# Layer 1's softplus in two parts, and one more sum step at its bias products

## The chip, the cores and the metric

The kernel runs on one core of one Trainium2 chip. The metric is the device time of one execution in microseconds; several executions of a kernel are timed and their median is compared. A core has five instruction queues that work side by side: TensorE (PE in the profile; its weight loads are PEld), VectorE (DVE), ScalarE (ACT), GpSimd (POOL) and SyncE (SP), which here only issues DMAs. Each takes its own instructions strictly in order and waits for the others through semaphores.

## The reference, cut to what matters

The program computes two residual layers on x, of shape (8, 256, 96, 96) in float32. Each layer first applies a group norm without weights, over groups of 8 channels. Layer 0 is an attention over channels in the Fourier domain. Layer 1, where the change is made, is a linear attention:

```python
def _L1_conv_ref(x, Wq, bq, Wk, bk, Wv, bv):
    xf = x.reshape(B, C, N)                                  # N = 9216 pixels
    q = softplus(einsum('dc,bcn->bnd', Wq, xf) + bq)         # d = 32
    k = softplus(einsum('dc,bcn->bdn', Wk, xf) + bk)
    v = einsum('ec,bcn->ben', Wv, xf) + bv
    attn_map = einsum('bdn,ben->bde', k, v)
    k_sum = sum(k, axis=-1) + 1e-6
    norm = 1.0 / einsum('bnd,bd->bn', q, k_sum)
    return einsum('bnd,bde,bn->ben', q, attn_map, norm)

x = x + _L0_conv_ref(_gn(x), ...)
x = x + _L1_conv_ref(_gn(x), ...)
```

The kernel never forms v. It forms k times the transposed x, with a column of ones for the sum of k, and applies the weights of v to that small matrix.

## The kernel before, in words

The eight images are worked off one after another in the loop at L1027, numbered from 0. An image goes through three stages. `images` applies the layer-0 attention to the rotated image, row block by row block, and adds the result to x. `layer1` does the group norm and all of layer 1 up to the small matrices. `output` forms the layer-1 result and stores it. In `output`, `attention` and `rotate` of the next image are mixed in.

A fifth activity runs beside these: `pair_sums` of the next image, a generator of 37 steps after its start. It loads x in a grouped layout, turns it by 32x32 blocks on VectorE (`turn_blocks`, L369), stores the turned rows to DRAM for a later stage (L372, SyncE, one store of 1536 KB for two turns), adds and subtracts row pairs (`pair`, L391 on GpSimd, L392 on VectorE for even pairs and on GpSimd for odd ones), and multiplies on TensorE into two accumulators (`products`, L343). A step is named (u, q): u counts row pairs from 0 to 12, q the three parts of a pair. The step (u, 0) also issues pair u + 1, and (u, 1) also issues turn u + 2, in both cases ahead of its own products. Turns with an even number write one half of the area of turned rows and those with an odd number the other half; the store behind each odd turn reads both halves. An odd turn also issues the loads of a later grouped block.

All engines run in the order in which the program text issues the instructions: the whole is built in a manual schedule, with no planner. `weave` (L929) sets how the sum steps fall in: a stage is a generator, and each number that it yields is the count of sum steps to be issued at that place (fractions are added up within a stage). `images` issues the start and 22 steps, so `layer1` begins with (7,1) and (7,2) in its group norm, and (8,0) between the two parts of the variance product. Image 7 is the last and has no sum steps.

`layer1` before the change, in its order:

- L773 to L787: group norm, weights of k and q scaled (`wkq`, L779 on ScalarE), bias products (`l1b`, L784 on TensorE), biases `bkqs` (L787 on VectorE).
- L805 to L822: projection. For each of six sets s, and for c = 0 (k) and c = 1 (q), 16 matmul instructions of 384 columns fill one PSUM tile that holds four column blocks of 32 channels. VectorE writes max(z, 0) (L814), ScalarE writes exp(-|z|) (L816 Abs, L817 Exp). In s = 1 VectorE also scales the weights of v (L821, L822).
- L829 to L844: `softplus(c, s)`. With e = exp(-|z|), softplus is max(z, 0) + log(1 + e). VectorE forms u = 1 + e (L834) and its rounding error (L835), ScalarE takes Ln of u (L836), VectorE subtracts the error (L837), and `close` adds the logarithm later (L843). softplus(0, 0) stands ahead of two sum steps and of the `bvs` product (L861).
- L864 to L891: for each set s, three transposes of k (`kT`, L867) and ScalarE's copy of them (L868), then softplus(0, s + 1); and for each of its three i, eight transposes of x into two PSUM tiles (`xT`, L878), their copies to SBUF (L881 on ScalarE, L883 on VectorE), `close`, and from s = 3 on softplus of q in two of the three. Twelve products `kx` (L850, two instructions each) for three i at a time accumulate k times x.
- L896 to L926: `kxs`, the transposed small matrices and the denominators, with three more sum steps, (9,0) to (9,2).

PSUM tiles of the name `ps` take turns in five buffers; a sixth tile waits until the first is read. All of `l1b`, `kq`, `bvs`, `kT` and `xT` are such tiles.

```python
        ex = y_of(b)[:, :, LO:LO + NS * CH]
...
            k, i = ((s // 2, s % 2) if s < 4 else (0, s - 2)) if c == 0 else ((1, s + 2) if s < 4 else (0, s))
```

`ex` holds e for k and q, `kq(c, s)` holds max(z, 0) and then the softplus, both in free space of the other image's area.

## Time and profile before

| | |
|---|---|
| median of 3 runs | 2661.95 us (2651.09 to 2665.03) |
| the profiled execution | 2650.85 us |
| its span, first to last instruction | 2649.0 us |
| mean granted TensorE clock | 0.984 |
| TensorE busy | 2509.3 us, 95% |
| VectorE busy | 1789.0 us, 68% |
| ScalarE busy | 1155.9 us, 44% |
| GpSimd busy | 865.6 us, 33% |
| `kq` products L812 | 127.9 us for the eight images |
| `xT` transposes L878 | 148.4 us |
| `kx` products L850 | 96.9 us (52.9, 23.9 and 20.1) |
| projection in image 0 | begins at 350.05 us |
| first `kT` and last `kx` in image 0 | 370.52 us and 403.03 us |

A line of a group gives line, engine, operation, output and inputs with the count, then the busy time and the mean in ns, then the idle time of the engine just before these instructions and what ended most of it. In a view in order of time, a line begins with start and duration in us and ends with the idle time before it and its releaser in brackets. In a table of windows the entries are the busy time of each engine with its instructions, then the granted share of TensorE's clock, the DMA share and GB/s. A busy TensorE is not a TensorE at its peak. Rows of one engine can overlap a little[...].

### The profile page before, as it was taken

Reading aid. Unit: us, or ns where it says so; the run is one execution under the profiler, and the core shown is the slowest. Engines: PE = TensorE matmul, PEld = TensorE weight load, DVE = VectorE, ACT = ScalarE, POOL = GpSimd, SP = SyncE. Lnnn points to the kernel's source line nnn. Section 1 sums busy time; section 2 is a strip of 40 time slices with the busy share of each in tenths; the row PEclk is TensorE's granted clock in tenths of the full one; section 3 lists DMA queues with packets and bytes.
Section 4 is the critical chain, followed back from the end, with each engine's and each line's share of the span. In section 5 each row is a group of like instructions: output and inputs, shape, how many; then the busy total and the mean of one; then the engine's idle time right before and its main releaser. Section 6 shows DMA issues by size and latency. Waiting matters only on the chain. (4 is left out here: it accounts for less than half of the span.)

```text
span 2649.0 us, 41157 instructions
## 1 busy us (share of the span) xinstructions
PE 2509.3 (95%) x15580; PEld 1730.2 (65%) x15580; DVE 1789.0 (68%) x3449; ACT 1155.9 (44%) x1985; POOL 865.6 (33%) x817
## 2 busy tenths in 40 slices
PE   3799999999999999999999999999999999999987
PEld 3775666757677576766668566685666757667544
DVE  3457866577756777568675686757866678766766
ACT  0035353453634526344353544435354353534554
POOL 2213514136042451324422343223523135141311
PEclk8899999999999999999999999999999999999999
DMA  9872628637195461935629264492636826286003
GB/s 210 238 216 60 166 71 270 205 67 189 40 313 161 106 173 57 315 120 143 153 90 305 80 167 129 159 316 42 166 89 230 245 60 179 58 289 210 1 7 144
DMA packets 282797, 413.27 MB, mean 156 GB/s; under 512 B 40772, under 2 KB 208872, under 8 KB 282600
## 3 DMA queue, kind: packets, MB, share of 16 engines
q1 hardware_dynamic: 274304, 406.16, 53.2%
q10 hardware_dynamic: 8296, 4.49, 0.8%
q8 instruction: 123, 2.02, 0.3%
q14 instruction: 74, 0.61, 0.1%
HBM read 256.72 MB, written 153.86 MB: 155 GB/s over the span
## 5 line engine op out<-in xcount | busy, mean ns | idle before, releaser
L710 PE MATMUL z<-arena,mz 128*128 128x384 f32 (+1 forms) x2304 | 593.4, 491 | 0.0
L718 PE MATMUL po<-e,wo 128*128 128x384 f32 x1536 | 527.6, 487 | 1.7 <-ACT e L755 1.7
L754 POOL TENSOR_TENSOR e<-e 128x768 f32<-128x768 f32 x192 | 348.4, 1815 | 552.7 <-ACT e L753 529.3
L343 PE MATMUL acc<-eo 128*128 128x257 f32 (+2 forms) x2368 | 437.1, 336 | 50.0 <-POOL eo L382 23.0
L343 PEld LDWEIGHTS acc<-eo 128*128 128x128 f32 (+1 forms) x2368 | 383.8, 194 | 143.9 <-issue 42.4
L710 PEld LDWEIGHTS z<-arena,mz 128*128 128x128 f32 (+1 forms) x2304 | 310.5, 164 | 236.0 <-issue 51.9
L718 PEld LDWEIGHTS po<-e,wo 128*128 128x128 f32 x1536 | 290.0, 190 | 204.7 <-ACT e L755 7.2
L749 DVE TENSOR_TENSOR e<-z,xT 128x768 f32<-128x768 f32 x384 | 361.9, 950 | 75.4 <-PE z L710 74.9
L647 PEld LDWEIGHTS y<-tm,arena 96*128 96x128 f32 x3072 | 365.9, 195 | 52.9 <-issue 18.9
L647 PE MATMUL y<-tm,arena 96*128 96x128 f32 x3072 | 385.7, 281 | 15.3 <-DMA arena<-xtd 6.4
L753 ACT ACTIVATE e<-e 128x1536 f32<-128x1536 f32 x192 | 284.5, 1482 | 195.2 <-DVE e L749 193.3
L391 POOL TENSOR_TENSOR eo<-arena 128x768 f32<-128x768 f32 x88 | 184.5, 2096 | 536.3 <-DVE arena L369 473.2
L720 DVE TENSOR_TENSOR arena<-arena,po 128x384 f32<-128x384 f32 x384 | 209.9, 553 | 190.0 <-PE po L718 190.0
L755 ACT ACTIVATE e<-e 128x768 f32<-128x768 f32 x192 | 162.0, 844 | 367.1 <-POOL e L754 363.2
L986 POOL TENSOR_TENSOR arena<-arena,po 128x384 f32<-128x384 f32 x180 | 179.1, 1014 | 224.0 <-ACT po L985 224.0
L369 DVE STREAM_TRANSPOSE arena<-arena 128x768 f32<-128x768 f32 x192 | 175.7, 953 | 32.5 <-DMA xtd<-arena 23.0
L299 DVE BATCH_NORM_STATS2 st<-arena 128x6 f32<-128x384 f32 x384 | 194.4, 548 | 0.0
L654 ACT COPY ys<-y 128x4 f32<-128x4 f32 (+1 forms) x200 | 32.4, 162 | 363.8 <-DVE arena L653 363.7
L878 PE MATMUL xT<-ident,arena 128*128 128x128 f32 x1152 | 148.4, 277 | 10.0 <-ACT xT L881 9.6
L878 PEld LDWEIGHTS xT<-ident,arena 128*128 128x128 f32 x1152 | 127.2, 142 | 32.0 <-issue 13.6
L985 ACT COPY po<-o 128x384 f32<-128x384 f32 x180 | 79.0, 485 | 157.4 <-PE o L977 152.4
L653 DVE COPY arena<-y 128x384 f32<-128x384 f32 (+1 forms) x200 | 109.1, 546 | 40.8 <-PE y L647 38.6
(225 smaller groups left out, 2493.1 us busy)
## 6 DMA issues: line engine op xcount, KB each, us to landing
xtd<-arena SPq DMA_DIRECT2D x48, 1536.0 KB
arena<-xtd SPq DMA_DIRECT2D x192, 384.0 KB
arena<-in_x_dram SPq DMA_DIRECT2D x96, 768.0 KB
out_dram<-arena SPq DMA_DIRECT2D x192, 384.0 KB
arena<-in_x_dram SPq DMA_DIRECT2D x376, 192.0 KB
tm<-rx SPq DMA_DIRECT2D x96, 159.0 KB
wl<-in_w1t_dram SPq DMA_DIRECT2D x8, 256.0 KB
wl<-in_w2t_dram SPq DMA_DIRECT2D x8, 256.0 KB
```

Of the source, the lines that this page charges most:

```text
L299: nc.vector.bn_stats(out=st[:, k, c, :], in_=x_of(b)[:, k, c * CH:(c + 1) * CH])
L343: nc.tensor.matmul(acc[c][:, m * (C + 1):m * (C + 1) + C + 1 - m * P], lhsT=eo[0:np_, q, c, 1 + m * P:1 + (m + 1) * P], rhs=eo[0:np_, q, c ...
L391: nc.gpsimd.tensor_add(e, ft, gt)
L647: nc.tensor.matmul(pu[:, o:o + P], lhsT=xt[:, s, k * P:(k + 1) * P], rhs=tm[:, n:n + P], start=True, stop=True)
L710: nc.tensor.matmul(out[:, 0:CH].rearrange("p (h q) -> p h q", q=PR), lhsT=columns(mz, k, c, j), rhs=yz[:, k, f, :, o:o + PR], start=(k == ...
L718: nc.tensor.matmul(po[:, 0:CH], lhsT=wo[:, k, m * P:(m + 1) * P], rhs=e[:, k, :], start=(k == 0), stop=(k == KC - 1))
L720: nc.vector.tensor_add(x[:, m, n], x[:, m, n], po[:, 0:CH])
L749: nc.vector.tensor_add(e[:, 2 * c:2 * c + 2, :].rearrange("p t (q h) -> p t q h", h=H), pz[:, 0:CH].rearrange("p (h q) -> p q h", h=H).uns ...
L753: nc.scalar.activation(e, e, AF.Square)
L754: nc.gpsimd.tensor_add(e[:, 0:2, :], e[:, 0:2, :], e[:, 2:4, :])
L878: nc.tensor.transpose(pt[:, j * C + k * P:j * C + (k + 1) * P], x[:, k, o:o + P], ident)
L986: nc.gpsimd.tensor_add(x[:, m, r], x[:, m, r], t)
```

## The change

The softplus is cut into `part` (all VectorE work but the last addition, now with the error subtracted from max(z, 0) at once) and `log` (ScalarE's Ln with bias 1, written over e). The temporary u is now VectorE's alone.

- The first parts of k move into the projection: `part(0, s - 1)` stands behind the two L814 of set s, and `part(0, 5)` behind the loop. `log(0, 0)` stands ahead of it. The small ScalarE instruction that made a zero bias goes away.
- The transposes of k move within a set: from ahead of its three i to the last one (i % 3 = 2), behind `close`, and ahead of that i's transposes of x. `log(0, s + 1)` follows the copy of kT on ScalarE, `part(1, s)`, the first part of q, follows on VectorE, and `log(1, s)` stands behind that i's copies. `close` is called once in a set.
- VectorE takes 12 of the 36 copies of `xT` in an image (the first tile of each i with i % 3 below 2), before 6.
- `layer1` yields one more sum step, between the scaling of `wkq` and the bias products. So every later sum step comes one place earlier, and one fewer is left for `output`.
- In `images` the yield is written the other way round, with the same values.

```diff
--- before.py
+++ after.py
@@ -758,7 +758,7 @@
             if len(pending) > 2:
                 project(*pending.pop(0))
             if i >= WI:
-                yield 2.5 if i > WI else 1
+                yield 1 if i == WI else 2.5
         for p in pending:
             yield 1
             project(*p)
@@ -777,6 +777,7 @@
         nc.sync.dma_start(out=wvs, in_=wvt.rearrange("(k p) o -> p k o", p=P))
         for k in range(KC):
             nc.scalar.activation(wkq[:, k], wkq0[:, k], AF.Copy, scale=rstd[:, k:k + 1])
+        yield 1
         pb = ps_tile(f"l1b_{b}")
         for c in range(2):
             for k in range(KC):
@@ -801,6 +802,14 @@
             k, i = ((s // 2, s % 2) if s < 4 else (0, s - 2)) if c == 0 else ((1, s + 2) if s < 4 else (0, s))
             o = LO + NS * CH + i * CH
             return y_of(b)[:, k, o:o + CH]
+
+        def part(c, s):
+
+            z, e = kq(c, s), ex[:, c, s * CH:(s + 1) * CH]
+            u = two.tile([P, CH], F32, tag="v16", name=f"spu_{b}_{c}_{s}")
+            nc.vector.tensor_scalar_add(u, e, 1.0)
+            nc.vector.scalar_tensor_tensor(u, in0=u, scalar=1.0, in1=e, op0=ALU.subtract, op1=ALU.subtract)
+            nc.vector.tensor_sub(z, z, u)
 
         for s in range(NS):
             n = slice(s * CH, (s + 1) * CH)
@@ -815,32 +824,26 @@
                                         op0=ALU.add, op1=ALU.max)
                 nc.scalar.activation(ex[:, c, n], ps[:, 0:CH], AF.Abs, bias=bkqs[:, c:c + 1])
                 nc.scalar.activation(ex[:, c, n], ex[:, c, n], AF.Exp, scale=-1.0)
+            if s:
+                part(0, s - 1)
             if s == 1:
                 nmb = own[:, 0:C].rearrange("p (k n) -> p k n", k=KC)
                 for k in range(KC):
                     nc.vector.tensor_scalar_mul(nmb[:, k, :], ones, nmean[:, k:k + 1])
                     nc.vector.tensor_scalar_mul(wvs[:, k, :], wvs[:, k, :], rstd[:, k:k + 1])
 
-        zero = own[:, 5 * C:5 * C + 1]
-        nc.scalar.activation(zero, ex[:, 1, NS * CH - 1:NS * CH], AF.Copy, scale=0.0)
-
         late = []
 
-        def softplus(c, s):
-
-            n = slice(s * CH, (s + 1) * CH)
-            z, e = kq(c, s), ex[:, c, n]
-            u = two.tile([P, CH], F32, tag="v16", name=f"spu_{b}_{c}_{s}")
-            nc.vector.tensor_scalar_add(u, e, 1.0)
-            nc.vector.scalar_tensor_tensor(e, in0=u, scalar=1.0, in1=e, op0=ALU.subtract, op1=ALU.subtract)
-            nc.scalar.activation(u, u, AF.Ln, bias=zero)
-            nc.vector.tensor_sub(z, z, e)
-            late.append((z, u))
+        def log(c, s):
+
+            e = ex[:, c, s * CH:(s + 1) * CH]
+            nc.scalar.activation(e, e, AF.Ln, bias=ones[:, 0:1])
+            late.append((kq(c, s), e))
 
         def close():
 
-            for z, u in late:
-                nc.vector.tensor_add(z, z, u)
+            for z, e in late:
+                nc.vector.tensor_add(z, z, e)
             late.clear()
 
         kx = acc_tile(f"kx_{b}")
@@ -854,22 +857,25 @@
         nc.gpsimd.memset(kring[:, :, :, C:C + 2], 1.0)
         slots = [*(xT[:, i] for i in range(4)), *kxt.pop(b), *(kring[:, i] for i in range(2))]
         pend = []
-        softplus(0, 0)
+        log(0, 0)
+        part(0, NS - 1)
         yield 2
         pv = ps_tile(f"bvs_{b}")
         for k in range(KC):
             nc.tensor.matmul(pv[:, 0:C], lhsT=nmb[:, k, :], rhs=wvs[:, k, :], start=(k == 0), stop=(k == KC - 1))
-        close()
         nc.vector.tensor_add(bvs, bvs, pv[:, 0:C])
         for s in range(NS):
-            pk = ps_tile(f"kT_{b}_{s}")
-            for i in range(CH // P):
-                nc.tensor.transpose(pk[:, i * P:(i + 1) * P], kq(0, s)[:, i * P:(i + 1) * P], ident)
-            nc.scalar.copy(kq(0, s), pk[:, 0:CH])
-            if s + 1 < NS:
-                softplus(0, s + 1)
             for i in range(s * CH // P, (s + 1) * CH // P):
                 xt = [slots[2 * (i % 4) + jj] for jj in range(2)]
+                if i % 3 == 2:
+                    close()
+                    pk = ps_tile(f"kT_{b}_{s}")
+                    for t in range(CH // P):
+                        nc.tensor.transpose(pk[:, t * P:(t + 1) * P], kq(0, s)[:, t * P:(t + 1) * P], ident)
+                    nc.scalar.copy(kq(0, s), pk[:, 0:CH])
+                    if s + 1 < NS:
+                        log(0, s + 1)
+                    part(1, s)
                 for jj in range(2):
                     pt = ps_tile(f"xT_{b}_{i}_{jj}")
                     for j in range(2):
@@ -877,17 +883,16 @@
                         for k in range(KC):
                             nc.tensor.transpose(pt[:, j * C + k * P:j * C + (k + 1) * P], x[:, k, o:o + P], ident)
                     src = pt.rearrange("p (j n) -> p j n", j=2)
-                    if jj or i % 6 > 1:
+                    if jj or i % 3 == 2:
                         nc.scalar.copy(xt[jj][:, :, 0:C], src)
                     else:
                         nc.vector.tensor_copy(xt[jj][:, :, 0:C], src)
-                close()
-                if s >= NS // 2 and i % (CH // P):
-                    softplus(1, 2 * s - NS + i % (CH // P) - 1)
-                if len(pend) == 3:
+                if i % 3 == 0:
                     for p in pend:
                         add_kx(*p)
                     pend = []
+                if i % 3 == 2:
+                    log(1, s)
                 pend.append((i, xt, kq(0, s)[:, i % (CH // P) * P:(i % (CH // P) + 1) * P]))
         close()
         for p in pend:
```

## The prediction

> **What bounds the kernel now.** I read the page first, then TensorE's waits, then layer 1 of image 0 on each engine in order of time, and last the granted clock. The page's busy times:

> ```profile
> PE 2509.3 (95%) x15580; PEld 1730.2 (65%) x15580; DVE 1789.0 (68%) x3449; ACT 1155.9 (44%) x1985; POOL 865.6 (33%) x817
> ```

> TensorE sets the time; only its 5% idle can be won. The waits of TensorE (us in total, times, longest) say where:

> ```profile
> PE acc L343 <- POOL eo L382: 23.0, 3, 15.1
> PE kT L867 <- DVE arena L843: 13.7, 16, 3.6
> ...
> PE xT L878 <- ACT xT L881: 9.6, 15, 1.0
> PE l1b L784 <- ACT wkq L779: 7.5, 8, 0.9
> ```

> The first is the program's head. The other three are layer 1: 31 us, 3.9 an image, are all that this change can touch there. The wkq wait is 0.93 us in every image; the kT wait is mostly 1.1 us ahead of the first transposes and 3.6 in image 7, which has no sum steps.

> The start of layer 1 in image 0, SyncE's queue and then TensorE's:

> ```profile
> 347.98 0.38 SPq L372 DMA_DIRECT2D xtd<-arena  x1
> ```
> ```profile
> 348.28 0.38 PE L325 MATMUL gv_b<-dv_b,gavg_sb 128*128 128x2 f32 x2
> 349.60 0.61 PE L784 MATMUL l1b<-nmean_b,wkq 128*32 128x1 f32 x32 [0.93 <-ACT wkq L779]
> 350.05 1.16 PE L812 MATMUL kq<-arena,wkq 128*32 128x384 f32 x12
> ```

> At 347.98 the 1536 KB store of the turned rows has just been issued. It matters because the added sum step brings the next turn forward to this place. That turn overwrites what the store reads:

> ```profile
> L369 DVE STREAM_TRANSPOSE arena<-arena 128x768 f32<-128x768 f32 x192 | 175.7, 953 | 32.5 <-DMA xtd<-arena 23.0 <-DMA arena<-in_x_dram 8.2
> ```

> VectorE between the projection and the first sets, where an addition opens each kT:

> ```profile
> 367.98 0.18 DVE L365 COPY arena<-wrap 128x16 f32<-128x16 f32 x1
> 368.18 1.84 DVE L369 STREAM_TRANSPOSE arena<-arena 128x768 f32<-128x768 f32 x2
> 369.95 0.52 DVE L843 TENSOR_TENSOR arena<-arena,spu 128x384 f32<-128x384 f32 x1
> ...
> 370.71 1.70 DVE L834 TENSOR_SCALAR spu<-arena 128x384 f32<-128x384 f32 x1
> ```

> And the clock in image 7 (the column before the last two), after TensorE stood 3.03 us (from 2549.36) and 3.61 us (from 2574.45):

> ```profile
> 2557.00:2560.00 3.00, 3.00 (x24) 0.98 (x20) 0.62 (x1) 1.38 (x2) 0.00 (x0) 0.50 0.00 0
> 2574.00:2578.00 4.00, 0.45 (x3) 0.04 (x1) 2.02 (x6) 3.20 (x5) 0.00 (x0) 0.93 0.00 0
> 2578.00:2581.00 3.00, 2.94 (x14) 2.94 (x15) 2.87 (x7) 1.28 (x3) 0.00 (x0) 0.52 0.00 0
> ```

> [...] half clock after gaps of 3.03 and 3.61 us. [...] L834 took 1.70 instead of 0.35 us while GpSimd's L391 ran (370.17 to 372.16). [...] Here the turn begins some 6 us after its store where it waits.

> **The change part by part** (image 0's clock; queues are walked in their order, each instruction starting when its engine is free and its inputs are done; VectorE's rows overlap their successors a little, so I use start to start: L814 0.56, a first part 0.38 + 0.60 + 0.47 = 1.45, PSUM copy 0.60, addition 0.47, its result after 0.55). The yields of images() keep their values: nothing.

> *Sum step at the bias products.* A step is 1.45 us of TensorE. It fills the 0.93 gap, so the projection begins at 350.56, not 350.05; one step fewer stays for the output stage, -1.45. But the step is (8,1), which puts turn 10 on VectorE ahead of the bias addition L787. The turn must wait for the store of 347.98, whose turn 9 belongs to a step only three steps earlier; before it had 20 us. Landing: the store's 1.5 MB show as five microseconds at 328 GB/s and 95% DMA share from 348.98, so the transposes start at about 354.1 (6.1 after issue; bounds 5.4 and 6.7) and end at 355.9. Behind them stand L787 and every L814, and ScalarE's Abs behind L814. TensorE writes four tiles of 1.29, stops 0.4 at the fifth (the fifth PSUM buffer still holds l1b) and 1.0 at the seventh, since ScalarE's first Exp loads its table (1.28) ahead of the second Abs. The projection ends at 367.4 (before 365.71).

> *k's first parts in the projection.* VectorE then needs 2 x 0.56 + 1.45 = 2.57 us per s, exactly TensorE's 2 x 1.287: a delay is never made good. From 356.1: 12 x 0.56 + 5 x 1.45 + 1.25 (nmb, wvs) + 0.86 (waiting for the first Exp) = 372.2. Then the last first part 1.45, pair 10's subtraction 0.85 (the step is now (9,0); the turn that stood here is gone), bias 0.35, two xT copies 1.20, addition 0.55: first kT at 376.6. ScalarE's Ln (table 1.28, 0.62) is done by 374.2 and no bound. The dropped zero instruction is worth nothing.

> *kT behind the i = 0, 1 transposes.* TensorE: 367.4 + 2 sum steps 2.9 + bvs 1.03 + four tiles of 0.465 = 373.2. It idles 3.4 us until 376.6.

> *close() behind VectorE's copy.* In every later set kT waits for an addition that is queued behind the copy of the previous i's first tile. From that tile's end on TensorE: 0.2 latency, copy 0.60, addition 0.55, 0.05 = 1.4, covered by the other tile, 0.465. So 0.95 us is lost per set, five times. The unstalled period is 4.54 (kT at 374.73, 379.21 and 383.75 before), so 5.5: last kT 376.6 + 27.5 = 404.1, then kT 0.33, two tiles 0.93, the last twelve kx products 1.5: 406.9. ScalarE needs 3.4 and VectorE 3.5 per set: no bound. The extra six VectorE copies for ScalarE's are in that.

> *q's softplus* no longer crowds the end, where before 5.58 instead of 4.54 us passed for s = 4 and waits stood in s = 5; L834 no longer meets L391. Those gains are inside the comparison with the measured end, 403.03: +3.8 in image 0. The other six ended 0.3 earlier: +4.1.

> *The other moved steps.* Turn 10 issues no DMA. Pair 10's L391 and memset come earlier on GpSimd, whose queue is otherwise empty there (idle from 351.8 to 370.2), and end near 358, before VectorE's first parts begin: nothing. Turn 11 takes pair 10's place behind kxs, ahead of ksum; the kse4 chain then ends as TensorE's sum step does: nothing, 0.3 if not covered. Its store leaves SyncE earlier and nothing new stands before it; the layer-0 weight loads and the middle row's store move one output step forward, ahead of output stores that no engine waits for there. The last step, (12,0), leaves the output loop one place earlier, which is bound by TensorE (0.93 of outputs and 1.45 of sums against 1.02 on VectorE): the full 1.45 comes back.

> Sum: 3.8 + 6 x 4.1 - 7 x 1.45 = 18.3. Image 7 has no sum step and no store: the same walk, before and after, gives +1.8 (kT 3.4 late plus 0.95 x 5, against its old waits). Clock: a 3.4 us gap like image 7's cost 24 transposes 3.62 instead of 2.86 and kT 0.4, 1.2 in all. The window need not fall on it (bounds 0 and 1.2): half, 7 x 0.6 = 4.2. Total 24.3. The profiled execution took 2650.85, giving 2675; against the runs' median, 2661.95, 2686.

> **Rivals.** *Nothing gained or lost*: turn 10's wait is absorbed, the store having landed early. Then the walk ends at 404.1, +1.1 to +1.4 an image, which the saved step cancels; with image 7, 2664. Against it: no store in the trace was seen to clear in under 5.4 us. *Faster*: the addition is not late at kT, because VectorE drains the copy while TensorE is held by something else. Five sets save 4.7 an image: 4.1 - 1.45 - 4.7 = -2.1, times seven, and -2.9 in image 7: 2645. It decides where the loss per set falls under about 0.4 us. For it: VectorE has a microsecond free per set. Against: that microsecond lies before the tile is written. *Much slower*: each image's gap brings 6.8 us at half clock as at 2553.6, which made image 7's projection 18.3 us for 15.7. 2.6 for 0.6, seven times, +14: 2700.

> **How the numbers follow.** Forecast 0.54, own range 2674 to 2699 (landing -5 and +4, clock -4 and +4, and the runs' own spread); nothing 0.20; faster 0.06; much slower 0.20. About 0.5% is what a measurement can tell from no change. From 2662 to 2706 leaves out the faster case, the low half of the neutral one and the top of the slow one. Faster 0.06, same 0.20, slower 0.74.

> **What would show it.** Right: l1b's wait gone; L369 with about 5 us more wait for xtd in each of seven images; kT's waits near 8 us an image, 3.4 of them at the first and 0.95 at each other; kT every 5.5 us; xT and kx waits near nothing; half clock in some layer-1 stretches. Wrong: kT every 4.6 us, or transposes at 349.6, would bring the time to before's or below.

## The result, and the profile after

The changed kernel took 2738.22 us (median of 4 runs, 2731.76 to 2740.67); the kernel before, run beside it, 2656.52 us (2648.99 to 2665.03). The ratio is 1.0303, 95% interval 1.0261 to 1.0344: 3% slower, beyond the upper end of the predicted range, 2706. The profiled execution took 2738.24 us, span 2736.4, so 87.4 us of span are to be explained.

First the page of the changed kernel: busy times, and the strips of TensorE's busy share and granted clock over 40 slices.

```profile
PE 2564.7 (94%) x15580; PEld 1786.7 (65%) x15580; DVE 1818.7 (66%) x3497; ACT 1130.9 (41%) x1929; POOL 864.0 (32%) x817
...
PE   4799989999899998999989999999999999899987
...
PEclk8899998999989999899998999999998999989998
```

TensorE issues the same 15580 instructions and is busy 55.4 us longer. Its instructions themselves got slower: the clock strip now dips again and again. This was it in the kernel before:

```profile
PEclk8899999999999999999999999999999999999999
```

The mean granted clock fell from 0.984 to 0.955, and the time spent at half clock within the span rose from 85 to 248 us.

The waits of TensorE after (total us, times, longest):

```profile
PE kT L874 <- DVE arena L846: 60.3, 48, 3.2
...
PE kq L821 <- ACT arena L825: 5.6, 7, 0.8
```

The `kT` wait grew from 13.7 to 60.3 us, and `l1b`'s wait of 0.93 an image went. To see where the rest is, I cut both traces into stages and took the mean of images 0 to 6, in us, with the half clock in it in brackets:

| stage | before | after | difference x 7 |
|---|---|---|---|
| `images`, up to the first `kq` | 171.8 (1.5) | 172.2 (1.9) | +3.3 |
| first `kq` to last `kx` | 52.7 (0) | 58.3 (3.9) | +39.2 |
| last `kx` to first output product | 12.6 (0) | 12.3 (0) | -1.6 |
| first to last output product | 38.2 (1.9) | 44.6 (19.0) | +44.9 |
| from there to the next image | 44.1 (0) | 44.1 (0) | 0 |

Image 7 adds 1.0 and the head 0.7; together 87.5. Half of the loss stands in the outputs, a stage that the change touches only by taking a sum step out of it.

Layer 1 of image 0 after, in order of time: SyncE's queue, VectorE, TensorE.

```profile
348.65 0.38 SPq L372 DMA_DIRECT2D xtd<-arena  x1
```
```profile
350.65 1.85 DVE L365 COPY arena<-wrap 128x16 f32<-128x16 f32 x1
354.71 1.84 DVE L369 STREAM_TRANSPOSE arena<-arena 128x768 f32<-128x768 f32 x2 [2.20 <-DMA arena<-in_x_dram]
...
382.39 0.69 DVE L889 COPY xT<-xT 128x512 f32<-128x512 f32 x1 [1.77 <-PE xT L884]
383.00 1.02 DVE L846 TENSOR_TENSOR arena<-arena 128x384 f32<-128x384 f32 x2
```
```profile
350.96 5.36 PE L821 MATMUL kq<-arena,wkq 128*32 128x384 f32 x64
356.65 2.84 PE L821 MATMUL kq<-arena,wkq 128*32 128x384 f32 x32 [0.33 <-DVE bkqs L788]
360.29 7.95 PE L821 MATMUL kq<-arena,wkq 128*32 128x384 f32 x96 [0.81 <-ACT arena L825]
...
376.67 0.90 PE L874 MATMUL kT<-ident,arena 128*128 128x128 f32 x3 [2.99 <-DVE arena L846]
...
383.69 0.52 PE L874 MATMUL kT<-ident,arena 128*128 128x128 f32 x3 [0.90 <-DVE arena L846]
...
389.32 0.52 PE L874 MATMUL kT<-ident,arena 128*128 128x128 f32 x3 [0.90 <-DVE arena L846]
```

Turn 10 starts 6.06 us after its store was issued; the projection stops twice, at its fifth and seventh tile; the first `kT` waits 2.99 us; every later one waits 0.90 us, for an addition (L846) that stands behind the copy (L889, 382.39) of a tile just transposed. The turn's line names a load as what ended its wait, because a load that was issued behind the store completed last before it (354.68). But the turn writes where the store reads; the store's own last completion came at 354.49, and in image 2 the first of these loads landed only after the turn had begun (1019.97 against 1019.88). So it is the store that the turn waits for. From the second set on `kT` comes every 5.63 us. From the first to the second it is 7.02, because the clock is halved from about 376 to 379.5.

The outputs of image 0 after: TensorE's queue around 437, then a table of windows (stretch, length; busy time and instructions of PE, PEld, DVE, ACT, POOL; granted clock; DMA share; GB/s).

```profile
434.97 0.92 PE L982 MATMUL o<-xT,own 32*128 32x384 f32 x6
436.67 0.91 PE L982 MATMUL o<-xT,own 32*128 32x384 f32 x2 [0.78 <-DMA out_dram<-arena]
437.78 3.79 PE L647 MATMUL y<-tm,arena 96*128 96x128 f32 x16 [0.20 <-ACT po L990]
```
```profile
434.14:437.55 3.41, 2.63 (x17) 1.30 (x15) 2.98 (x10) 1.45 (x5) 2.15 (x3) 1.00 1.07 399
437.55:458.00 20.45, 20.14 (x91) 15.38 (x92) 7.36 (x22) 6.74 (x17) 8.14 (x9) 0.50 0.75 247
```

At 437.55 the clock falls, although TensorE was busy for 2.63 of the 3.41 us before, and its longest stop there was 0.78 us (436.67). Then it stays at half for 20.45 us with TensorE 98% busy (20.14): sixteen rotation products take 3.79 us, where 2.05 is their time at full clock (a line of that is shown below). In image 0 of the kernel before, the clock falls at about the same place (18.3 us into the outputs, with one step more ahead of it; 16.2 here), but for 3.4 us only.

### The profile page after: what moved, and what is told of

Its sections match the earlier page's. It is cut to its first block, busy times and chain, and to the rows that moved or that the text cites. A ratio compares the mean times of both kernels' runs of the same rounds, so it can differ in the third digit from the quotient of the medians.

```text
span 2736.4 us, 41129 instructions
## 1 busy us (share of the span) xinstructions
PE 2564.7 (94%) x15580; PEld 1786.7 (65%) x15580; DVE 1818.7 (66%) x3497; ACT 1130.9 (41%) x1929; POOL 864.0 (32%) x817
## 3 DMA queue, kind: packets, MB, share of 16 engines
q8 instruction: 123, 2.02, 0.3%
## 5 line engine op out<-in xcount | busy, mean ns | idle before, releaser
L343 PE MATMUL acc<-eo 128*128 128x257 f32 (+2 forms) x2368 | 438.2, 337 | 50.2 <-POOL eo L382 23.1
L343 PEld LDWEIGHTS acc<-eo 128*128 128x128 f32 (+1 forms) x2368 | 384.7, 194 | 140.8 <-issue 42.2
L647 PEld LDWEIGHTS y<-tm,arena 96*128 96x128 f32 x3072 | 398.8, 209 | 61.4 <-issue 29.8
L647 PE MATMUL y<-tm,arena 96*128 96x128 f32 x3072 | 421.7, 297 | 13.2 <-DMA arena<-xtd 7.2
L391 POOL TENSOR_TENSOR eo<-arena 128x768 f32<-128x768 f32 x88 | 183.6, 2086 | 484.9 <-DVE ksum L909 293.6
L369 DVE STREAM_TRANSPOSE arena<-arena 128x768 f32<-128x768 f32 x192 | 175.7, 954 | 49.2 <-DMA xtd<-arena 32.1
L884 PEld LDWEIGHTS xT<-ident,arena 128*128 128x128 f32 x1152 | 137.3, 148 | 17.7 <-issue 16.5
```

The source lines that it names most:

```text
L343: nc.tensor.matmul(acc[c][:, m * (C + 1):m * (C + 1) + C + 1 - m * P], lhsT=eo[0:np_, q, c, 1 + m * P:1 + (m + 1) * P], rhs=eo[0:np_, q, c ...
L391: nc.gpsimd.tensor_add(e, ft, gt)
L647: nc.tensor.matmul(pu[:, o:o + P], lhsT=xt[:, s, k * P:(k + 1) * P], rhs=tm[:, n:n + P], start=True, stop=True)
L884: nc.tensor.transpose(pt[:, j * C + k * P:j * C + (k + 1) * P], x[:, k, o:o + P], ident)
```

## The experiments

The theory from these traces: **two separate losses**. In layer 1 the walk of the prediction holds; in the outputs a stretch with too little TensorE work drops the clock for five or six windows of 3.4 us. The rival: the half clock comes with the added step or with layer 1's pauses, and goes when these go. The table gives every run; "layer 1" is first `kq` to last `kx` and "outputs" first to last output product, each the mean of images 0 to 6 in us, "long" is the number of these seven images with 13.7 us or more at half clock in the outputs. These three columns come from the one profiled execution of each kernel, the median and the ratio from all its runs; the kernel before ran anew beside each group of runs, and the ratio is to that.

| kernel | median us | ratio to before (interval) | layer 1 | outputs | long |
|---|---|---|---|---|---|
| before | | | 52.7 | 38.2 | 0 |
| the change | 2738.22 | 1.0303 (1.0261 to 1.0344) | 58.3 | 44.6 | 7 |
| a: step alone | 2695.15 | 1.0168 (1.0138 to 1.0198) | 54.0 | 42.8 | 5 |
| b: split alone | 2703.31 | 1.0198 (1.0173 to 1.0223) | 57.1 | 41.7 | 4 |
| c: outputs filled | 2689.12 | 1.0146 (1.0131 to 1.0161) | 58.1 | 36.7 | 0 |
| d: step out of layer 1 | 2699.29 | 1.0182 (1.0163 to 1.0200) | 57.7 | 40.0 | 1 |
| e: c, earlier addition | 2635.63 | 0.9907 (0.9881 to 0.9933) | 52.2 | 36.7 | 0 |
| f: b, both moves | 2610.07 | 0.9809 (0.9779 to 0.9839) | 49.2 | 37.3 | 0 |
| g: rotation later | 2742.18 | 1.0308 (1.0259 to 1.0356) | 58.2 | 39.9 | 4 |
| h: e, last first part later | 2616.66 | 0.9838 (0.9810 to 0.9867) | 49.7 | 36.7 | 0 |
| i: fill in layer 1 | 2697.14 | 1.0149 (1.0094 to 1.0205) | 56.6 | 39.9 | 3 |
| j: f, steps shifted | 2681.47 | 1.0083 (1.0054 to 1.0112) | 49.2 | 37.3 | 0 |
| k: half the fill | 2704.49 | 1.0177 (1.0120 to 1.0235) | 58.2 | 38.8 | 2 |
| l: c, step later | 2688.72 | 1.0117 (1.0080 to 1.0154) | 58.0 | 37.2 | 0 |
| m: fill inside the stretch | 2714.14 | 1.0209 (1.0174 to 1.0243) | 58.2 | 40.0 | 0 |
| n: both moves, step kept | 2647.32 | 0.9954 (0.9930 to 0.9978) | 49.8 | 39.6 | 3 |

**a, the sum step alone.** The kernel before with one line:

```diff
             nc.scalar.activation(wkq[:, k], wkq0[:, k], AF.Copy, scale=rstd[:, k:k + 1])
+        yield 1
         pb = ps_tile(f"l1b_{b}")
```

> The kernel before with the one more sum step alone, softplus as it was. Theory 1 (output stage): the sum step that is missing from the output stage lets TensorE's clock fall to half there for 17 to 20 us in each of seven images; then the output stage takes 44 to 45 us instead of 37 to 39, layer 1 some 2 us more (turn 10 waits for its store), and the time is about 2656 + 7 x 9 = 2720 to 2730. Theory 2 (layer 1): the pauses of 3.0 and 5 x 0.9 us that the split softplus puts before kT bring the low clock on, also later; here they are not made, so the output stage keeps 37 to 39 us and the time is 2655 to 2670.

Layer 1 took 54.0 instead of 52.7: the earlier turn, with its wait for the store, costs 1.3 us an image. The outputs ran long at half clock in five of seven images. One line that saves TensorE work in the outputs is enough to make the kernel 1.7% slower.

**b, the split alone.** The changed kernel without that line, so that its outputs hold the same steps as before:

```diff
-        yield 1
         pb = ps_tile(f"l1b_{b}")
```

> The changed kernel without the one more sum step. Theory 1: the output stage is as before (37 to 39 us, at most 3.4 us at half clock), only layer 1 is longer, by 3 to 5 us an image: 2680 to 2695. Theory 2: the pauses before kT stay (about 3 us at the first, 0.9 at each other), so the output stage is at half clock for 17 to 20 us as in the changed kernel: 2730 to 2745.

Layer 1 takes 57.1 without any store wait in it. But the outputs, with the steps of before, run long at half clock in four of seven images. The missing step is therefore not the only thing that brings the long half clock; a and b also don't add up to the change (1.68 and 1.98% against 3.03%).

**c, the outputs filled.** Four products of the sizes of a full sum step (128 rows, 257 and 129 columns) at the place where the last step, (12,0), stood in the kernel before. Their result is read by nobody; they are work on top, and nothing is left out. The same holds for e, h, i, k, l and m.

```diff
                         finish(sums)
+                        if 2 * s + m == 4:
+                            fill = ps_tile(f"fill_{b}")
+                            wf = wo.rearrange("p k n -> p (k n)")
+                            for i in range(4):
+                                nc.tensor.matmul(fill[:, 0:C + 1 - i % 2 * P], lhsT=wf[:, 0:P],
+                                                 rhs=wf[:, 0:C + 1 - i % 2 * P], start=True, stop=True)
                         next(mixed)
```

> The changed kernel with four matrix products of the sizes of a sum step (their result is not used) at the place in the output stage from which the sum step has gone. Theory 1: the clock stays up in the output stage, the half-clock stretch goes to 0 to 3.4 us an image and the time falls by 7 x (9 - 1.5) to about 2685. Theory 2: the output stage stays at half clock for 17 us and the fill adds 7 x 1.5: about 2748.

More work made the kernel faster: its span is 49.0 us shorter (2687.4 instead of 2736.4). Its windows at the same place, columns as above:

```profile
435.18:438.60 3.42, 3.42 (x27) 2.62 (x25) 2.99 (x9) 1.33 (x6) 1.97 (x3) 1.00 1.08 395
438.60:459.00 20.40, 19.63 (x160) 14.49 (x159) 11.61 (x34) 10.71 (x28) 11.82 (x13) 1.00 1.03 355
```

TensorE is busy through the whole window, the clock doesn't fall, and in the next 20.4 us 160 matmul instructions fit in where 91 did. The outputs take 36.7 us in all seven images instead of 44.6: 7 x 7.9 = 55 us, of which `images` and image 7 give back 3 each. Layer 1 is untouched at 58.1, so the two losses are separate.

**d, eight steps left as before, the added one taken out of layer 1.**

```diff
         part(0, NS - 1)
-        yield 2
+        yield 1
         pv = ps_tile(f"bvs_{b}")
```

> The changed kernel with one of the two sum steps ahead of the bvs product taken away, so that layer 1 has eight again and the output stage has all that it had before; turn 10 still stands at the bias products. Theory 1: output stage as before, layer 1 3 to 5 us longer: 2680 to 2695. Theory 2: as the changed kernel, 2730 to 2745.

With the outputs' steps restored, six images have 3.4 us at half clock and one has 20.5. Between b and c: the content matters, and something else too.

**g, the next image's rotation later,** by one output step, so about where the missing step had put it.

```diff
                         finish(sums)
-                        next(mixed)
-                        next(mixed)
+                        if 2 * s + m > 4:
+                            next(mixed)
+                            next(mixed)
```

> The changed kernel with the attention and the rotation of the next image mixed in one place later in the output stage, at the place where they stood before, and no products in the place of the sum step that has gone. If it is their order against the outputs and the stores that brings the clock down, the half-clock stretch of the output stage goes (0 to 3.4 us an image) and the time is about 2680. If it is the missing work of TensorE, the stretch stays at 17 us or more and the time is 2730 to 2745.

Four images still run long, with the fall some 3.5 us later; in the other three the outputs shorten to 34.9, but what was put off comes back behind them (48.5 instead of 44.1). Nothing is won.

**e, the addition ahead of the copies.** c, with `close` one i earlier, so that VectorE's two additions of logarithms stand before the copy that held them up:

```diff
-                if i % 3 == 2:
+                if i % 3 == 1:
                     close()
+                if i % 3 == 2:
                     pk = ps_tile(f"kT_{b}_{s}")
```

> The kernel with the filled output stage, with close() of the two additions moved from behind VectorE's copy of i % 3 = 1 to ahead of it. Theory of the prediction: the 0.9 us waits before kT of the later sets go, the sets come every 4.6 us instead of 5.6, layer 1 is 5.1 us shorter in all eight images and the time is about 2689 - 41 = 2648. Rival: the sets stay at 5.3 us or more since VectorE or ScalarE is the bound, and the time is above 2675.

TensorE's waits of e and its queue in image 0:

```profile
PE kT L875 <- DVE arena L846: 19.4, 8, 2.6
```
```profile
382.99 0.49 PE L875 MATMUL kT<-ident,arena 128*128 128x128 f32 x3
...
387.52 0.49 PE L875 MATMUL kT<-ident,arena 128*128 128x128 f32 x3
```

Of 48 waits only the 8 first ones remain, the period is 4.53 again, and layer 1 falls from 58.1 to 52.2. The span is 55.7 us shorter than c's: 41 in these layers, 9 in image 7 and 5 in `images`. That shows the queue place of the addition to be the whole of the loss per set: 5 x (5.63 - 4.53) = 5.5 of these 5.9.

**h, k's last first part behind the first `kT`.** e, with

```diff
         log(0, 0)
-        part(0, NS - 1)
         yield 2
...
                         log(0, s + 1)
+                    if s == 0:
+                        part(0, NS - 1)
                     part(1, s)
```

> The same, and k's last first part (three VectorE instructions, 1.45 us) moved from ahead of the sum steps to behind the first kT. The pause before the first kT shrinks from 3 us to about 1, and if that pause is what puts layer 1 at half clock for 3.4 us, this goes too: 8 x (1.45 + 1.2) less, about 2627. If the low clock in layer 1 has another cause, 8 x 1.45 less: 2636.

The wait at the first `kT` went from 2.4 to 1.5 us an image, and with it the half-clock window behind it. The window of e behind its first `kT`, then that of h:

```profile
377.56:380.97 3.41, 3.41 (x22) 2.85 (x24) 2.53 (x6) 2.80 (x6) 0.00 (x0) 0.50 0.00 0
```
```profile
376.00:379.40 3.40, 3.22 (x39) 2.71 (x43) 3.26 (x8) 2.77 (x7) 0.00 (x0) 1.00 0.00 0
```

39 instructions against 22 in the same time. Layer 1 takes 49.7: of the 2.5 us, 1.0 is the earlier first `kT` and the rest the clock.

**f, both moves without step and fill.** b with the edits of e and h.

> The split alone (no added sum step, no products to fill) with both moves: early close() and k's last first part behind the first kT. Layer 1 by the walk 3.7 us shorter than in the kernel before in each of eight images: 2622 if the output stages keep their clock, and up to 7 x 8 us more, 2678, if they fall on the same stretch of half clock as four of seven did with the split alone.

This is the fastest kernel of all, 2610.07 us, 1.9% below the kernel before. Its waits and two of its `kT`:

```profile
PE kT L873 <- DVE arena L845: 16.4, 8, 2.4
...
PE l1b L784 <- ACT wkq L779: 7.5, 8, 0.9
```
```profile
374.47 0.52 PE L873 MATMUL kT<-ident,arena 128*128 128x128 f32 x3 [2.01 <-DVE arena L845]
...
379.05 0.52 PE L873 MATMUL kT<-ident,arena 128*128 128x128 f32 x3
```

The split itself is worth 3.5 us an image in layer 1 (52.7 to 49.2) once its two bad queue places are mended. Its outputs hold the same instructions as b's, yet have no half clock at all in seven images. That is 37.3 against 41.7 us, so some 30 of its gain over b come from the clock in the outputs.

**n, both moves with the step kept.** The changed kernel with the edits of e and h, no fill.

> The changed kernel with early close() and k's last first part behind the first kT, the added sum step kept, nothing filled. Layer 1 falls by 8 us an image as with the fill (58.3 to about 50 us). If the output stage's fall is a matter of its own content and its place against the clock's windows, the images now meet the windows elsewhere and some keep the clock: 2600 (none falls) to 2665 (all fall). If layer 1's pauses are what brings it about, none falls: 2605.

Layer 1 takes 49.8 with no half clock, so its pauses are gone. Still three of seven outputs run long at half clock. The rival that layer 1's pauses bring it falls. The times of 18 runs spread from 2620.27 to 2668.03, more than those of any other kernel here; in this trace, long outputs come in images 0, 4 and 6 only.

**i, the fill in layer 1 instead.** The changed kernel with the four products of c ahead of the `bvs` product:

```diff
         yield 2
+        fill = ps_tile(f"fill_{b}")
...
         pv = ps_tile(f"bvs_{b}")
```

> The changed kernel with the four products of the filled kernel put not into the output stage but into layer 1, ahead of the bvs product, where TensorE pauses for 3 us anyway. If it is the work at its place in the output stage that keeps the clock up there, the output stages stay at half clock for 17 to 20 us and the time stays at 2725 to 2740, less the 1.2 us an image of layer 1's own half-clock window if the shorter pause takes that away. If any work, or only a shift in time, is enough, it falls to about 2690.

The half clock behind the first `kT` is gone in all seven images (56.6 with 1.4 us of added work in it), where that work takes up part of the pause. Long outputs remain in three.

**k, half the fill.** c with two products in place of four, 0.7 us:

```diff
-                            for i in range(4):
+                            for i in range(2):
```

> The filled kernel with two of the four products (257 and 129 columns, half the work). If the clock hangs on the amount of work in one stretch, half of it leaves some images at half clock: 2690 to 2730. If any interruption of the outputs is enough, the time is as with all four less 7 x 0.7: about 2684.

Five outputs without half clock, two with 17.1 us. A partial remedy.

**m, the fill inside the stretch.** c with the four products two output steps later:

```diff
-                        if 2 * s + m == 4:
+                        if 2 * s + m == 6:
```

> The changed kernel with the same four products one set later in the output stage, behind the place where the clock falls, so inside the stretch at half clock. If full-width products raise the clock again, the stretch ends within one or two windows of them, 7 to 10 us instead of 17 to 20, and the time is 2738 - 7 x 4 + 7 x 1.5 = about 2720. If the clock hangs on what precedes the fall alone, the stretch keeps its 17 us or more: 2740 to 2755.

The clock falls where it did, 16.4 to 17.2 us into the outputs, but it comes back after 6.8 us in six images and 3.4 in one. TensorE's queue of m in image 0, where it does so after 3.4:

```profile
440.06 3.10 PE L647 MATMUL y<-tm,arena 96*128 96x128 f32 x16 [0.20 <-ACT po L990]
...
444.49 1.58 PE L1009 MATMUL fill<-wo 128*128 128x257 f32 x8
...
449.31 2.05 PE L647 MATMUL y<-tm,arena 96*128 96x128 f32 x16
```

Rotation products take 3.10 us ahead of the added ones, part of it at half clock, and 2.05 behind them. Products of 128 rows and 257 or 129 columns, 1.4 us of them, end what 20 us of a full queue of 32-row outputs and 96-row rotations did not.

**l, the step behind the projection instead.** c without the step at the bias products, and `yield 3` for `yield 2`. Turn 10 then waits for nothing.

```diff
-        yield 1
         pb = ps_tile(f"l1b_{b}")
...
-        yield 2
+        yield 3
```

> The filled kernel with the added sum step behind the projection (three there) and none at the bias products, so that turn 10 comes 20 us after its store. Theory of the prediction: the waits in the projection go (1.1 us an image), the 0.93 us gap at the bias products comes back, the first kT stands 1.3 us nearer to the start of the projection and layer 1's end 0.8 us earlier in seven images: 2689 - 6 = 2683. If the turn's wait for its store cost more than the walk says, it falls further, below 2675.

The medians of l and c lie 0.4 us apart; by the ratios l is 0.3% lower, but the intervals overlap. Layer 1 takes 58.0 in l, with the step's 1.45 us now inside it, with `l1b`'s wait of 0.93 back and the `kq` waits gone; 58.1 in c. So what the filled gap saves and what the wait for the store costs are about the same. a gave the second as 1.3 us. The turn starts 6.06 us after the store's issue and VectorE stands still for 2.20 of them, the most visible new wait of the change; little more than one reaches TensorE.

**j, f with the steps shifted by one.** f with `yield 1` at the bias products, and one step less in the first block of `images` so that the outputs keep their steps:

```diff
-                yield 1 if i == WI else 2.5
+                yield 0 if i == WI else 2.5
```

> The split with early close() and the late first part, and a sum step at the bias products that comes from images() (which yields none at its first place instead of one), so that the step there is (8,0), which brings no turn, and the output stage keeps its steps. Theory: the 0.93 us gap goes without a new wait, 1.2 us an image less than without it, 2602 if the clock in the output stage stays up. If the missing step in images() opens a gap there, or the clock falls, 2610 or more.

A miss. `images` takes 181.6 us instead of 171.3; TensorE waits there for a pair sum that is now late, and the clock adds 8.8 us at half:

```profile
PE acc L343 <- DVE eo L388: 53.9, 8, 11.6
```

That wait was 12.3 us, once, in f.

| kernel | no half clock in the outputs | 3.4 us only | 13.7 us or more |
|---|---|---|---|
| *steps as before* | | | |
| before | 0.82 to 1.28 | 2.19 to 2.34 | |
| b | 0.79, 3.07 | 3.17 | 2.87 to 3.00 |
| d | | 3.23 to 3.34, 0.11 to 0.20 | 2.61 |
| f | 0.67 to 2.01 | | |
| j | 0.80 to 1.85 | | |
| *one step less* | | | |
| the change | | | 0.70 to 0.97, 2.71 |
| a | | 3.30, 0.05 | 2.95, 3.11, 0.12 to 0.41 |
| i | 1.20 to 2.02 | | 2.50 to 3.01 |
| n | 1.51 to 2.10 | | 2.28 to 3.09 |
| *one step less, filled* | | | |
| c | 0.61 to 0.99 | | |
| e | 0.79 to 1.45 | | |
| h | 1.51 to 2.07, 2.95 | | |
| l | 0.40, 0.47, 3.04 to 3.39 | 2.66, 2.76 | |
| *other outputs* | | | |
| k | 0.46 to 0.88 | | 0.22, 0.23 |
| g | 0.06, 0.07, 2.80 | | 0.75 to 0.92, 2.74 |

m's images, at 0.29 to 0.67 and 3.30, fell for 6.8 and 3.4 us.

Within one kernel, whose images all hold the same instructions, the place on the grid decides, sharply: in n 2.10 gives none and 2.28 long, in k 0.46 and 0.23, in b 3.07 and 3.00. Between the groups the content counts. Where all but one of the change's images start, 0.70 to 0.97, nearly the same places give no half clock with the steps as before (nine images between 0.67 and 0.95) nor with the fill (c and e). With the steps as before, long half clock stands only between 2.61 and 3.00; with one step less between 2.28 and 3.11 and between 0.12 and 0.97; with the fill nowhere. So the missing step widened the part of the grid where the clock falls, and the change's images lie in the part that it added. b falls with its steps kept, in the four images that lie at 2.87 to 3.00. f escapes by its places, 0.67 to 2.01, not by its outputs. All this was read from one trace of each kernel; no run shifted the place alone.

## Why the prediction was wrong

**Direction and layer 1.** "Slower" was right. Against the prediction's walk in image 0: the turn 6.06 us after its store (6.1 predicted), stops at the fifth and seventh tile 0.33 and 0.81 (0.4 and 1.0), the first `kT` at 376.67 (376.6), its wait 2.99 (3.4), each later wait 0.90 (0.95), period 5.63 (5.5). Two of the mechanisms named are confirmed by a run of their own: the late addition by e, the first part ahead of the first `kT` by h. The wait for the store is read from the trace. The 376.67 is in part luck: the turn began at 354.71, 0.6 later than walked, and VectorE's work behind it came out 0.5 shorter. (The walk's 379.21 and 383.75 for the kernel before are starts of weight loads; the products began at 379.32 and 383.85, which leaves the period as it is.) "The change part by part" put +3.8 and 6 x 4.1 on layer 1, with 4.2 for the clock: 32.6 us. The stages up to the first output product show 3.3 + 39.2 - 1.6 = 40.9. Of the 8.3 missing, 0.13 x 5 x 7 = 4.5 is the period; the rest is mainly the clock behind the first `kT`: 7.02 - 5.63 = 1.4 in image 0, where 0.6 was taken, an estimate: half of the 1.2 of image 7. (In i, without half clock there, the first period is 5.66.) Image 7 gave +1.0 for 1.8.

**Where it failed.** The step is "the last step, (12,0), leaves the output loop ... the full 1.45 comes back". Its arithmetic is nearly right where the clock holds: n's outputs without half clock take 36.09, those of before 37.30, 1.2 less. But in the changed kernel that stage took 44.6 instead of 38.2, +44.9 in place of -10.2. That is 55 of the 63 us by which the sum, 24.3, was too small, and c took it away by adding products at that one place, with its images at places on the grid where the change's fall. The prediction put what the step was worth to the clock at nothing.

The sum's clock term has the same fault. It took image 7's two stops, 3.03 and 3.61 us, as the pattern, asked where else TensorE would stand for 3 us and found layer 1 only. That was the author's estimate, and the changed kernel's trace disagrees: the clock fell at 437.55 behind a window whose longest stop was 0.78 us. The sign of it was in the kernel before, and the sum made no use of it. Its windows (columns as above) in image 0's outputs:

```profile
434.00:438.00 4.00, 3.78 (x19) 2.42 (x18) 1.23 (x4) 1.01 (x3) 0.76 (x1) 0.59 1.07 400
438.00:442.00 4.00, 3.90 (x33) 3.23 (x34) 1.32 (x6) 2.55 (x7) 1.95 (x2) 1.00 1.06 357
```

The clock was already at half for 3.4 us there, in four of seven images, and a sum step was to be taken out of this stage.

**The rivals.** "Nothing gained or lost" and "faster" had layer 1 wrong. "Much slower" had the right cause, the clock, in the wrong stage (the projection) and of the wrong size, 14 us instead of some 60: 19.0 us of half clock in the outputs of each image make them 44.6 - 36.1 = 8.5 us longer.

**Still open.** What in TensorE's work the clock follows. The added products of c and m have 128 rows, the outputs 32 and the rotations 96, but no run changed the rows alone or the density of the issue alone; which of them counts, if either, is not shown. Why the place on the grid decides as it does is open too.

## What to carry to other kernels

Ask of work that is taken out of a stage what it did for the clock there: print the granted clock by stage before the change, and treat a stage that already drops for one window (3.4 us in image 0's outputs before) as one that may drop for six (20.45 us after). Look at the queue place of a small operation that others wait for: moving the two additions of `close` ahead of one copy was worth 5.9 us an image, the most of anything in layer 1. And mend a change before dropping it: the split lost 2% as made and won 1.9% with two of its pieces moved. Part of that win hangs on where its outputs lie on the clock's grid: with b's long outputs in it, 30 us more, an estimate gives 0.7%.

## What the runs showed of the hardware that I had not expected

- **The clock falls without an idle window.** The sixteen traces, cut into windows of 3.413 us, show 194 falls in images 0 to 6. In the window ahead of each, TensorE's queue was at most 89% busy, in 80 of them over 80%; and many windows below 90% bring no fall: of those at full clock from image 0's projection to the end of image 6, 77 in the kernel before and 94 in the changed one, 7 and 19 were followed by one. Image 7, with no other image's work beside its outputs, is different: in eight traces a fall follows a window that was 94 to 100% busy. In h it held products of 32 rows alone:

```profile
2580.79 12.05 PE L984 MATMUL o<-arena,own 32*128 32x384 f32 x53 [0.63 <-DVE arena L964]
```
```profile
2582.18:2585.60 3.42, 3.42 (x18) 2.06 (x17) 3.42 (x9) 0.64 (x2) 1.78 (x2) 1.00 0.35 130
2585.60:2589.01 3.41, 3.41 (x18) 3.38 (x16) 3.01 (x7) 0.96 (x2) 1.42 (x3) 0.50 1.05 389
```

The busy share is not the work done, though: at half the clock the next window holds 18 products too.

- **It can stay low on a busy queue.** The change's outputs stay at half clock for 17 to 20.5 us, five or six windows of 3.413 us, in image 0 with TensorE 98% busy (20.14 of 20.45).
- **Images can repeat their place on the grid, and with it their falls.** From one start of the outputs to the next, the change's images 2 to 5 take 331.0 to 331.2 us (96.96 to 97.04 windows) and images 0 to 2 of the kernel before 320.9 (94.0), so the next outputs start at nearly the same place. n's first three take 323.3, 318.0 and 313.6 us (94.7, 93.2 and 91.9 windows), and its places wander. Whether the half clock itself pulls images onto the grid is not shown.
- **A 128x16 copy took 1.85 us** (L365 at 350.65) instead of 0.18, beside GpSimd's L392 from 350.55 to 352.38. One copy in each of images 0 to 6 of the changed kernel is as slow, 1.75 to 1.86 us, and each began 0.10 to 0.12 us after an L392. In the kernel before, 21 such copies had an L391 begin 0.01 to 0.10 us after them and took 0.18 to 0.19 us. What holds the slow ones is not shown.
